# Multiplying the dense tiles of a graph layer in pairs, by halves of columns, and spreading the second products

## The chip, the cores and the metric

The kernel runs on one core of one Trainium2 chip. The metric is the device time of the whole program in microseconds (us). Before the change it is 1784.06 us, the median of three runs (1779.79 to 1784.26).

## What is computed

Two graph layers over N = 2500 nodes with 1024 features and E = 80000 edges, sorted by destination. Both layers see the same edges.

```python
edge_index = jnp.stack([src, dst])
h = jnp.maximum(_layernorm(x, axis=-1), 0.0)
x = x + _L0_gnn_ref(h, L0_gnn_W, edge_weight, src, dst)
h = jnp.maximum(_layernorm(x, axis=-1), 0.0)
x = x + _L1_gnn_ref(h, edge_index, L1_gnn_W, L1_gnn_b)
```

Layer 0 is `support = h @ W`, and then for every edge `support[src]` times its weight, summed by `dst`. Layer 1 is `h @ W.T + b`, and then a sum over the edges and a loop at each node, each scaled by the inverse roots of the degrees of its two ends. All is float32.

## The kernel before

Nodes are cut into 20 tiles of 128 rows. `direct` (L47) works in three stages.

**First stage (up to L526).** Support is multiplied tile by tile on TensorE (`product`, L278) and stored to DRAM. In between the edges are counted (`count_group`, L416): one-hot matrices on VectorE (L436, L438), small bf16 products on TensorE (L440), added to a count matrix per tile of destinations (L448). A tile's counts (20 x 128 x 128 numbers of 16 bits) are stored by SP to `cnat` (L497), and a fresh `counts` buffer is cleared by ScalarE (L422); there are three such buffers. For the first four tiles (`DENSE = 4`; those with most edges) the edge weights are summed in the same way into a matrix `dense[t]` that stays in SBUF.

**Middle stage (L527 to L668).** It forms the sums of layer 0. The 16 thin tiles are gathered (`gathered`, L564): for each block of 128 edges POOL gathers 128 rows of support by an indirect DMA into a buffer `msg` (L569), VectorE makes a one-hot `oh_r` (L573), ScalarE the rounded weighted rows `hi` (L575), VectorE the rest `lo` (L577), and TensorE takes four products (L581). There are 378 such blocks. The four dense tiles are multiplied (`multiplied`, L590): for each of the 20 tiles k of support POOL loads its rows (L595) into a `msg` buffer, and TensorE takes two products of `dense[t]`, one for each half of the columns (L597). `msg` has eight buffers in all, for gathers and dense rows together, and POOL issues in program order.

When a tile's sum is complete, `finish` (L540) adds x to it, stores the sum to DRAM (`x1_d`, L544), normalises it (`normed`, L137), transposes it on TensorE (L534, copied from the PSUM tile `pT` by ScalarE at L535) and multiplies it by the second weights (L554, 16 products, the "second products"), adds the bias (L558) and stores the result to `hid_d` (L561). `finish` is a generator of 12 pieces.

The order is written out by hand. `plan` (L608 to L621) is a list of steps, True for a dense step and False for a block of gathers: `OPENING = 8` dense steps first, and then for each thin tile its blocks with a share of the dense steps among them, two kept for the tile's end; the dense steps end 48 blocks before the end. The tiles come in the order of `ORDER`, so the dense ones as 3, 2, 1, 0. The loop at L640 takes one step after the other, loads the second weights (L646, eight loads of 512 KB on SP) in the first eight steps after the opening, and takes pieces of the tiles that wait in `waiting` at a rate fixed for each thin tile (L620). After each step `count` (L501) may add counting work, from rough costs per engine (`takes`, L467). A framework then lays down one instruction order for each engine and the waits between them; each engine runs its order strictly.

PSUM has two buffers each of `mm` (the sums of a tile, two banks), of `pT` and of `cb` (counts). The tiles of `xt` and `hn` have two buffers each.

**Last stage (from L671).** The degrees, and then for each of the 20 tiles the sum over all tiles of `hid_d` with the transposed counts (L725).

Of the kernel before, what the change touches and what calls it, by code (L numbers as in the profile page):

```python
# [9 lines left out]
F32 = mybir.dt.float32  # L10
# [9 lines left out]
P = 128  # L20
# [7 lines left out]
TILE_BLOCKS = (146, 62, 48, 41, 36, 33, 30, 28, 27, 25, 24, 23, 22, 21, 21, 20, 20, 19, 19, 10)  # L28
# [4 lines left out]
DENSE = 4  # L33
# [4 lines left out]


OPENING = 8  # L40
TAIL = 48

ORDER = (3, 4, 5, 6, 2, 7, 8, 9, 1, 10, 11, 12, 13, 0, 14, 15, 16, 17, 18, 19)
# [3 lines left out]
def direct(  # L47
# [26 lines left out]
    nc = tc.nc  # L74
    N, D = x.shape
    E = src.shape[0]
    NT = -(-N // P)
    KC = D // P
    H = D // 2
# [9 lines left out]
    def rows(t):  # L89
        return min(P, N - t * P)  # L90
# [3 lines left out]
    support = dram.tile([N, D], F32, name="support")  # L94
    cnat = dram.tile([NT, NT, P, P], F16, name="cnat")
    x1_d = [dram.tile([P, D], F32, name=f"x1_d{t}") for t in range(NT)]
# [22 lines left out]
    work = first.enter_context(tc.tile_pool(name="work", bufs=2))  # L119
    psum = first.enter_context(tc.tile_pool(name="psum", bufs=2, space=bass.MemoryType.PSUM))  # L120
# [26 lines left out]
    def load_rows(t, pool):  # L147
        xt = pool.tile([P, D], F32, name="xt")
        if rows(t) < P:
            nc.vector.memset(xt, 0.0)  # L150
        nc.sync.dma_start(xt[:rows(t), :], x[t * P:t * P + rows(t), :])
        return xt
# [69 lines left out]
    start = prep.tile([NT, 1], F32, name="start")  # L222
# [28 lines left out]
    for c in range(QC):  # L251
        n = min(P, NBP - c * P)
# [13 lines left out]
    def on_pe(i):  # L266
        nonlocal last_pe
        last_pe = i
        if len(fences) >= BEHIND and fences[-BEHIND] is not None:
            order_behind(i, fences[-BEHIND])  # L270
        return i
# [27 lines left out]
    for i, to in enumerate((row_p, src_p, wgt_p)):  # L299
        for c0 in range(0, QC, 4):  # L300
            ps = psum.tile([P, 4, P], F32, name="pT")
            m = min(4, QC - c0)
            for c in range(c0, c0 + m):
                n = min(P, NBP - c * P)
                if i == 2:
                    v = got[:n, c, :, 2].bitcast(F32)
                else:
                    v = got_f[:n, i, c, :]
# [7 lines left out]
            for c in range(c0 + whole, c0 + m):  # L316
                n = NBP - c * P
# [11 lines left out]
    for t in range(2, NT):  # L329
        n = TILE_BLOCKS[t] // 2  # L330
        v = second[:, K0[t] - K0[2]:K0[t] - K0[2] + 2 * n].rearrange("p (n g) -> p n g", g=2)
# [81 lines left out]
    dense = {}  # L413
# [53 lines left out]
    def takes(pe=0.0, v=0.0, s=0.0):  # L467
        for i, us in enumerate((pe, v, s)):
            clock[i] += us
        clock[PE] = max(clock[PE], clock[V] - LEAD, clock[S] - LEAD)  # L470
        for i in (V, S):
            clock[i] = max(clock[i], clock[PE] - LEAD)
# [40 lines left out]
    def count_all(t):  # L513
        for queue in to_count:
            while any(g[0] == t for g in queue):
                count_next(queue)
# [13 lines left out]
    def transposed(v, into):  # L530
        for k0 in range(0, KC, 4):
            pT = psum.tile([P, 4, P], F32, name="pT")
            for k in range(4):
                nc.tensor.transpose(pT[:, k, :], v[:, (k0 + k) * P:(k0 + k + 1) * P], ident)  # L534
            nc.scalar.copy(into[:, k0:k0 + 4, :], pT)  # L535
            yield 0.7, 0.0, 0.6

    PIECES = 12

    def finish(t, sums):  # L540

        xt = load_rows(t, work)
        nc.vector.tensor_add(xt, sums.rearrange("p h d -> p (h d)"), xt)  # L543
        nc.sync.dma_start(x1_d[t], xt)  # L544
        yield 0.0, 1.25, 0.0
        hn = normed(xt, work)
        yield 0.0, 2.2, 1.5
        vT = work.tile([P, KC, P], F32, name="vT")
        yield from transposed(hn, vT)
        hid = work.tile([P, D], F32, name="hn")  # L550
        for h in range(2):
            mm = psum.tile([P, 4, P], F32, name="pT").rearrange("p a b -> p (a b)")
            for k in range(KC):
                on_pe(nc.tensor.matmul(mm, vT[:, k, :], w1_sb[k][:, h * H:(h + 1) * H],  # L554
                                       start=(k == 0), stop=(k == KC - 1)))
                if k % 2 and k < KC - 1:
                    yield 1.75, 0.0, 0.0
            nc.vector.tensor_add(hid[:, h * H:(h + 1) * H], mm, bias[:, h * H:(h + 1) * H])  # L558
            if h == 0:
                yield 1.75, 0.65, 0.0  # L560
        nc.sync.dma_start(hid_d[t], hid)  # L561
        yield 1.75, 0.65, 0.0

    def gathered(t, sums):  # L564
        n = TILE_BLOCKS[t]
        for j in range(n):
            k = K0[t] + j
            msg = gpool.tile([P, D], F32, name="msg", bufs=8)
            nc.gpsimd.indirect_dma_start(  # L569
                out=msg, out_offset=None, in_=support,  # L570
                in_offset=bass.IndirectOffsetOnAxis(ap=src_p[:, k:k + 1], axis=0))
            oh = gpool.tile([P, P], F32R, name="oh_r", bufs=3)
            nc.vector.tensor_scalar(oh, iota, row_p[:, k:k + 1], None, op0=ALU.is_equal)  # L573
            hi = gpool.tile([P, D], F32R, name="hi")
            nc.scalar.activation(hi, msg, AF.Copy, scale=wgt_p[:, k:k + 1])  # L575
            lo = gpool.tile([P, D], F32R, name="lo")
            nc.vector.scalar_tensor_tensor(lo, msg, wgt_p[:, k:k + 1], hi.bitcast(F32),  # L577
                                           op0=ALU.mult, op1=ALU.subtract)
            for v in (hi, lo):
                for h in range(2):  # L580
                    i = nc.tensor.matmul(  # L581
                        sums[:, h, :], oh, v[:, h * H:(h + 1) * H],
                        start=(j == 0 and v is hi), stop=(j == n - 1 and v is lo))
                    if v is hi and h == 0:
                        on_pe(i)
            yield 0.92, 1.47, 1.16

    last_load = None

    def multiplied(t, sums):  # L590
        nonlocal last_load
        count_all(t)
        for k in range(NT):
            msg = gpool.tile([P, D], F32, name="msg", bufs=8)
            last_load = nc.gpsimd.dma_start(msg[:rows(k), :], support[k * P:k * P + rows(k), :])  # L595
            for h in range(2):
                i = nc.tensor.matmul(  # L597
                    sums[:, h, :], dense[t][:rows(k), k, :], msg[:rows(k), h * H:(h + 1) * H],
                    start=(k == 0), stop=(k == NT - 1))
                if h == 0:  # L600
                    on_pe(i)
            yield 1.75, 0.0, 0.0

    thick, thin = [t for t in ORDER if t < DENSE], [t for t in ORDER if t >= DENSE]
    blocks = sum(TILE_BLOCKS[t] for t in thin)
    plan = [True] * OPENING  # L608
    rate = [0.0] * OPENING
    done = 0  # L610
    for t in thin:
        n = TILE_BLOCKS[t]
        done += n
        m = min(DENSE * NT, OPENING + -(-(DENSE * NT - OPENING) * done // (blocks - TAIL))) - sum(plan)
        inner = max(m - 2, 0)
        for j in range(n):
            plan.append(False)
            plan += [True] * ((j + 1) * inner // n - j * inner // n)
        plan += [True] * (m - inner)
        rate += [1.1 * PIECES * (1 + m / NT) / (n + m)] * (n + m)  # L620
    assert sum(plan) == DENSE * NT  # L621

    waiting = []
    todo = left(to_count[1])
    w1_sb = []

    def steps_of(tiles):
        for t in tiles:
            sums = psum.tile([P, 2, H], F32, name="mm")
            n = NT if t < DENSE else TILE_BLOCKS[t]  # L630
            for j, took in enumerate((multiplied if t < DENSE else gathered)(t, sums)):
                if j == n - 1:
                    rest = finish(t, sums)
                    takes(*next(rest))
                    waiting.append(rest)
                yield took

    kinds = {True: steps_of(thick), False: steps_of(thin)}
    pieces = 0.0
    for i, is_dense in enumerate(plan):  # L640
        took = next(kinds[is_dense])
        if i == OPENING:
            for k in range(KC):
                w1_sb.append(wpool.tile([P, D], F32, name=f"w{k}"))
        if i >= OPENING and (i - OPENING) < KC:
            order_behind(nc.sync.dma_start(w1_sb[i - OPENING], w1t[(i - OPENING) * P:(i - OPENING + 1) * P, :]),  # L646
                         last_load)
        if i == OPENING + KC:
            nc.sync.dma_start(bias, b1.rearrange("(o d) -> o d", o=1).to_broadcast([P, D]))
        pieces = min(pieces + rate[i], 2.0) if waiting else 0.0  # L650
        while pieces >= 1 and waiting:
            piece = next(waiting[0], None)
            if piece is None:
                waiting.pop(0)
                continue
            takes(*piece)
            pieces -= 1
        count(*took, least=todo * (1 - 1.05 * (i + 1) / len(plan)))
    for steps in kinds.values():
        for _ in steps:  # L660
# [2 lines left out]
        while queue:  # L663
            count_next(queue)
    store_counts(late=False)
    for rest in waiting:
        for _ in rest:
            pass  # L668

# [401 lines left out]
```

## Time and profile before

| What | Value |
|---|---|
| Median of three runs | 1784.06 us |
| The profiled execution, its own time | 1785.47 us |
| Its span | 1783.5 us |
| TensorE busy | 1675.6 us (94%) |
| VectorE busy | 1205.6 us (68%) |
| ScalarE busy | 903.1 us (51%) |
| POOL busy | 537.5 us (30%) |
| Middle stage, from the first dense product to the first product of the last stage | 476.0 to 1398.7 us |
| TensorE, VectorE, POOL busy in the middle stage | 857.7, 760.4, 517.9 us of 922.7 |
| Moved by DMA in the middle stage | 282 MB, 305 GB/s |
| Mean granted TensorE clock, whole span | 0.978 |

A line of a group of instructions gives the source line, the engine, the operation, what is written and read, the shape and the count, and then the busy time and the mean duration of one. A float32 product of 512 columns is recorded as two. "Idle before" is the time the engine had nothing to run ahead of these instructions, with what ended it. In the chain of waits each row is a start, a duration and what ran, followed back from the last instruction of the program to what released it.

### The profile page before, as it was taken

What the parts mean: (1) busy time and instruction counts of PE and PEld (TensorE: products, weight loads), DVE (VectorE), ACT (ScalarE), POOL (GpSimd) and SP (SyncE); (2) the same over time, 40 slices, a digit from 0 to 9 for tenths busy, and PEclk for the clock granted to TensorE, in tenths of its full rate; (3) what the DMA queues carried; (4) which work ended last, traced back from release to release, by engine and by line L of the source; (5) the groups of instructions that cost most, each with busy time, mean ns of one, the idle gap of its engine ahead of it and who ended that gap; (6) DMA issues with size and microseconds to landing.
All of it is one profiled execution on the core that took longest, in us unless ns stands there. A gap on an engine that the chain in (4) does not pass through costs nothing. (4 is left out here: it accounts for less than half of the span.)

```text
span 1783.5 us, 21221 instructions
## 1 busy us (share of the span) xinstructions
PE 1675.6 (94%) x6506; PEld 1039.3 (58%) x6506; DVE 1205.6 (68%) x3051; ACT 903.1 (51%) x1476; POOL 537.5 (30%) x537
## 2 busy tenths in 40 slices
PE   6999999999978998998999889999999999999997
PEld 2465555544345555554555545555565568888886
DVE  5888888898779887788999898777787420000000
ACT  3499999961156655455555444555564431111110
POOL 3000000000257755565656545555562000000000
PEclk9999999999989999999999999999999999999999
DMA  7513122132689988898889888988986773342420
GB/s 248 200 38 94 54 78 60 40 96 71 210 306 358 347 306 280 294 332 277 321 306 337 283 289 266 356 309 316 318 300 215 224 197 93 90 102 80 113 62 32
DMA packets 217424, 369.94 MB, mean 207 GB/s; under 512 B 115758, under 2 KB 135224, under 8 KB 217302
## 3 DMA queue, kind: packets, MB, share of 16 engines
q0 software_dynamic: 66160, 240.22, 38.5%
q1 hardware_dynamic: 151142, 128.29, 23.7%
q8 instruction: 53, 0.87, 0.2%
q14 instruction: 69, 0.57, 0.1%
HBM read 300.79 MB, written 54.56 MB: 199 GB/s over the span
## 5 line engine op out<-in xcount | busy, mean ns | idle before, releaser
L575 ACT ACTIVATE hi<-msg,wgt_p 128x1024 fp32r<-128x1024 f32 x378 | 426.4, 1147 | 359.8 <-PE mm L581 272.7
L569 POOL DMA_INDIRECT msg<-support,src_p x378 | 477.0, 1262 | 325.6 <-DVE lo L577 130.6
L577 DVE SCALAR_TENSOR_TENSOR lo<-msg,wgt_p,hi 128x1024 fp32r<-128x1024 f32 x378 | 478.9, 1280 | 79.4 <-ACT hi L575 47.2
L281 PE MATMUL mm<-w,hT 128*128 128x512 f32 x640 | 317.2, 608 | 2.4 <-ACT hT L173 2.4
L581 PE MATMUL mm<-hi,oh_r 128*128 128x512 f32 x756 | 292.6, 468 | 13.4 <-ACT hi L575 11.5
L554 PE MATMUL pT<-w,vT 128*128 128x512 f32 x640 | 301.3, 593 | 0.0
L581 PE MATMUL mm<-lo,oh_r 128*128 128x512 f32 x756 | 279.3, 450 | 18.3 <-DVE lo L577 18.1
L445 ACT ACTIVATE wl<-oh_low,wpart 128x128 bf16<-128x128 bf16 x891 | 261.8, 403 | 0.0
L725 PE MATMUL mm<-lo,bT 128*128 128x512 f32 (+1 forms) x800 | 248.3, 393 | 3.8 <-DVE lo L699 3.7
L725 PE MATMUL mm<-hi,bT 128*128 128x512 f32 (+1 forms) x800 | 247.9, 392 | 3.1 <-ACT bT L707 2.0
L713 DVE SCALAR_TENSOR_TENSOR rows<-mm,dis,rows 128x1024 f32<-128x1024 f32 x20 | 25.7, 1284 | 307.9 <-PE mm L725 307.9
L581 PEld LDWEIGHTS mm<-lo,oh_r 128*128 128x128 f32 x756 | 139.5, 194 | 102.2 <-DVE lo L577 55.6
L581 PEld LDWEIGHTS mm<-hi,oh_r 128*128 128x128 f32 x756 | 143.1, 193 | 95.4 <-issue 44.9
L438 DVE TENSOR_SCALAR oh_key<-iota,key 128x200 bf16<-128x200 f16 (+12 forms) x675 | 195.1, 292 | 3.0 <-PE cb L452 2.8
L597 PE MATMUL mm<-msg,dense 128*128 128x512 f32 (+1 forms) x320 | 164.4, 631 | 30.1 <-DMA msg<-support 29.6
L707 ACT CAST bT<-cT 128x2560 fp32r<-128x2560 f16 x20 | 46.6, 2335 | 261.2 <-PE mm L725 257.7
L554 PEld LDWEIGHTS pT<-w,vT 128*128 128x128 f32 x640 | 120.5, 189 | 94.7 <-issue 81.3
L725 PEld LDWEIGHTS mm<-lo,bT 128*128 128x128 f32 (+1 forms) x800 | 149.7, 188 | 39.8 <-DVE lo L699 9.0
L725 PEld LDWEIGHTS mm<-hi,bT 128*128 128x128 f32 (+1 forms) x800 | 150.4, 189 | 36.5 <-ACT bT L707 2.4
L436 DVE TENSOR_SCALAR oh_low<-iota,low 128x128 bf16<-128x128 f16 x675 | 168.7, 254 | 3.5 <-PE cb L440 2.2
L448 DVE TENSOR_TENSOR counts<-cb,counts 128x200 f32 (+13 forms) x296 | 138.8, 470 | 41.7 <-PE cb L440 35.4
L281 PEld LDWEIGHTS mm<-w,hT 128*128 128x128 f32 x640 | 109.2, 195 | 65.1 <-issue 59.3
(142 smaller groups left out, 1189.5 us busy)
## 6 DMA issues: line engine op xcount, KB each, us to landing
msg<-support POOLq DMA_DIRECT2D x76, 512.0 KB, 7.1
xt<-in_x SPq DMA_DIRECT2D x38, 512.0 KB, 6.6
cnat<-counts SPq DMA_DIRECT2D x20, 640.0 KB, 9.3
x_d<-xt SPq DMA_DIRECT2D x20, 512.0 KB, 6.5
hid_d<-hn SPq DMA_DIRECT2D x20, 512.0 KB, 6.3
rows<-hid_d SPq DMA_DIRECT2D x20, 512.0 KB, 4.4
rows<-x_d SPq DMA_DIRECT2D x20, 512.0 KB, 4.0
hT<-in_xT SPq DMA_DIRECT2D x19, 512.0 KB, 4.2
```

Source lines behind the costliest of these rows:

```text
L281: on_pe(nc.tensor.matmul(mm[:, h, :], vT[:, k, :], ws[k][:, h * H:(h + 1) * H], start=(k == 0), stop=(k == KC - 1)))
L436: nc.vector.tensor_scalar(oh_low, iota16[:, :P], low[:, k:k + 1], None, op0=ALU.is_equal)
L438: nc.vector.tensor_scalar(oh_key[:, :NT * w], iota16[:, :NT * w], key[:, k:k + 1], None, op0=ALU.is_equal)
L445: nc.scalar.activation(wl[:, i, :], oh_low, AF.Copy, scale=wpart[:, i, k:k + 1])
L448: nc.vector.tensor_tensor(to, cb[:, :NT * w].rearrange("p (t w) -> p t w", w=w), to, op=ALU.add)
L554: on_pe(nc.tensor.matmul(mm, vT[:, k, :], w1_sb[k][:, h * H:(h + 1) * H], start=(k == 0), stop=(k == KC - 1)))
L569: nc.gpsimd.indirect_dma_start(out=msg, out_offset=None, in_=support, in_offset=bass.IndirectOffsetOnAxis(ap=src_p[:, k:k + 1], axis=0))
L575: nc.scalar.activation(hi, msg, AF.Copy, scale=wgt_p[:, k:k + 1])
L577: nc.vector.scalar_tensor_tensor(lo, msg, wgt_p[:, k:k + 1], hi.bitcast(F32), op0=ALU.mult, op1=ALU.subtract)
L581: i = nc.tensor.matmul(sums[:, h, :], oh, v[:, h * H:(h + 1) * H], start=(j == 0 and v is hi), stop=(j == n - 1 and v is lo))
L597: i = nc.tensor.matmul(sums[:, h, :], dense[t][:rows(k), k, :], msg[:rows(k), h * H:(h + 1) * H], start=(k == 0), stop=(k == NT - 1))
L725: nc.tensor.matmul(mm[:, h, :], bT[:rows(k), k, :], v[:rows(k), h * H:(h + 1) * H], start=(k == ORDER[0] and v is his[k]), stop=(k == ORDE ...
```

## The change

Dense tiles are taken in pairs, (3, 2) and then (1, 0). For each half of the columns, one `sums` tile in PSUM holds both tiles' halves; POOL loads two tiles of support rows, half as wide, into one `msg` buffer (for the last two, where rows are fewer, in two loads), and each loaded row is multiplied by both tiles' matrices. At the end of each half x is loaded in halves, added, and stored to `x1_d` in halves. The normalising of these tiles loads `x1_d` again.

`finish` ends with the transposes, and the second products become a generator of their own, `second_rows`. The loop takes second products at a rate set anew for each thin tile from what is pending, and, apart from that, parts of the next tile's normalising (`preparing`) at most every second step. The plan puts 20 dense steps, not 16, before the end of the first thin tile.

```diff
@@ -38,6 +38,7 @@
 
 
 OPENING = 8
+BESIDE = 12
 TAIL = 48
 
 ORDER = (3, 4, 5, 6, 2, 7, 8, 9, 1, 10, 11, 12, 13, 0, 14, 15, 16, 17, 18, 19)
@@ -535,18 +536,27 @@
             nc.scalar.copy(into[:, k0:k0 + 4, :], pT)
             yield 0.7, 0.0, 0.6
 
-    PIECES = 12
-
-    def finish(t, sums):
-
-        xt = load_rows(t, work)
-        nc.vector.tensor_add(xt, sums.rearrange("p h d -> p (h d)"), xt)
-        nc.sync.dma_start(x1_d[t], xt)
-        yield 0.0, 1.25, 0.0
+    PIECES = 8
+
+    def finish(t, sums=None):
+
+
+        if sums is None:
+            xt = work.tile([P, D], F32, name="xt")
+            nc.sync.dma_start(xt, x1_d[t])
+        else:
+            xt = load_rows(t, work)
+            nc.vector.tensor_add(xt, sums.rearrange("p h d -> p (h d)"), xt)
+            nc.sync.dma_start(x1_d[t], xt)
+            yield 0.0, 1.25, 0.0
         hn = normed(xt, work)
         yield 0.0, 2.2, 1.5
         vT = work.tile([P, KC, P], F32, name="vT")
         yield from transposed(hn, vT)
+        products_left.append(second_rows(t, vT))
+
+    def second_rows(t, vT):
+
         hid = work.tile([P, D], F32, name="hn")
         for h in range(2):
             mm = psum.tile([P, 4, P], F32, name="pT").rearrange("p a b -> p (a b)")
@@ -587,57 +597,91 @@
 
     last_load = None
 
-    def multiplied(t, sums):
-        nonlocal last_load
-        count_all(t)
-        for k in range(NT):
-            msg = gpool.tile([P, D], F32, name="msg", bufs=8)
-            last_load = nc.gpsimd.dma_start(msg[:rows(k), :], support[k * P:k * P + rows(k), :])
-            for h in range(2):
-                i = nc.tensor.matmul(
-                    sums[:, h, :], dense[t][:rows(k), k, :], msg[:rows(k), h * H:(h + 1) * H],
-                    start=(k == 0), stop=(k == NT - 1))
-                if h == 0:
-                    on_pe(i)
-            yield 1.75, 0.0, 0.0
+    def multiplied(ts):
+
+
+        nonlocal last_load, pending
+        for t in ts:
+            count_all(t)
+        for h in range(2):
+            sums = psum.tile([P, 2, H], F32, name="mm")
+            cols = slice(h * H, (h + 1) * H)
+            for k0 in range(0, NT, 2):
+                msg = gpool.tile([P, 2, H], F32, name="msg", bufs=8)
+                if rows(k0 + 1) == P:
+                    last_load = nc.gpsimd.dma_start(
+                        msg, support[k0 * P:(k0 + 2) * P, cols].rearrange("(k p) d -> p k d", p=P))
+                else:
+                    for k in (k0, k0 + 1):
+                        last_load = nc.gpsimd.dma_start(msg[:rows(k), k - k0], support[k * P:k * P + rows(k), cols])
+                for k in (k0, k0 + 1):
+                    for i, t in enumerate(ts):
+                        m = nc.tensor.matmul(sums[:, i, :], dense[t][:rows(k), k, :], msg[:rows(k), k - k0],
+                                             start=(k == 0), stop=(k == NT - 1))
+                        if i == 0:
+                            on_pe(m)
+                    if k == NT - 1:
+                        xt = work.tile([P, 2, H], F32, name="xt")
+                        for i, t in enumerate(ts):
+                            nc.sync.dma_start(xt[:, i], x[t * P:(t + 1) * P, cols])
+                        nc.vector.tensor_add(xt, sums, xt)
+                        for i, t in enumerate(ts):
+                            nc.sync.dma_start(x1_d[t][:, cols], xt[:, i])
+                        takes(v=1.25)
+                        if h == 1:
+                            stored.extend(ts)
+                            pending += PIECES * len(ts)
+                    yield 1.75, 0.0, 0.0
+
 
 
 
     thick, thin = [t for t in ORDER if t < DENSE], [t for t in ORDER if t >= DENSE]
     blocks = sum(TILE_BLOCKS[t] for t in thin)
     plan = [True] * OPENING
-    rate = [0.0] * OPENING
+    stretch = [0] * OPENING
     done = 0
     for t in thin:
         n = TILE_BLOCKS[t]
         done += n
-        m = min(DENSE * NT, OPENING + -(-(DENSE * NT - OPENING) * done // (blocks - TAIL))) - sum(plan)
+        begun = OPENING + BESIDE
+        m = min(DENSE * NT, begun + -(-(DENSE * NT - begun) * (done - TILE_BLOCKS[thin[0]])
+                                      // (blocks - TAIL - TILE_BLOCKS[thin[0]]))) - sum(plan)
         inner = max(m - 2, 0)
         for j in range(n):
             plan.append(False)
             plan += [True] * ((j + 1) * inner // n - j * inner // n)
         plan += [True] * (m - inner)
-        rate += [1.1 * PIECES * (1 + m / NT) / (n + m)] * (n + m)
+        stretch += [n + m] + [0] * (n + m - 1)
     assert sum(plan) == DENSE * NT
 
-    waiting = []
+    waiting, stored, products_left = [], [], []
+    pending = 0
     todo = left(to_count[1])
     w1_sb = []
 
-    def steps_of(tiles):
+    def blocks_of(tiles):
+        nonlocal pending
         for t in tiles:
             sums = psum.tile([P, 2, H], F32, name="mm")
-            n = NT if t < DENSE else TILE_BLOCKS[t]
-            for j, took in enumerate((multiplied if t < DENSE else gathered)(t, sums)):
-                if j == n - 1:
+            for j, took in enumerate(gathered(t, sums)):
+                if j == TILE_BLOCKS[t] - 1:
                     rest = finish(t, sums)
                     takes(*next(rest))
                     waiting.append(rest)
+                    pending += PIECES
                 yield took
 
-    kinds = {True: steps_of(thick), False: steps_of(thin)}
-    pieces = 0.0
+    def rows_of(tiles):
+        for i in range(0, DENSE, 2):
+            yield from multiplied(tiles[i:i + 2])
+
+    kinds = {True: rows_of(thick), False: blocks_of(thin)}
+    pieces = rate = parts = 0.0
+    preparing = None
     for i, is_dense in enumerate(plan):
+        if stretch[i]:
+            rate = min(pending - (3 if i + stretch[i] < len(plan) else 0), 14) / stretch[i]
         took = next(kinds[is_dense])
         if i == OPENING:
             for k in range(KC):
@@ -647,14 +691,22 @@
                          last_load)
         if i == OPENING + KC:
             nc.sync.dma_start(bias, b1.rearrange("(o d) -> o d", o=1).to_broadcast([P, D]))
-        pieces = min(pieces + rate[i], 2.0) if waiting else 0.0
-        while pieces >= 1 and waiting:
-            piece = next(waiting[0], None)
-            if piece is None:
-                waiting.pop(0)
-                continue
-            takes(*piece)
-            pieces -= 1
+        pieces = min(pieces + rate, 2.0)
+        while pieces >= 1 and products_left:
+            takes(*next(products_left[0]))
+            pieces, pending = pieces - 1, pending - 1
+            if pending % PIECES == 0:
+                assert next(products_left.pop(0), None) is None
+        parts = min(parts + 0.7, 1.0)
+        if parts == 1 and preparing is None and len(products_left) < 2 and (waiting or stored):
+            preparing = waiting.pop(0) if waiting else finish(stored.pop(0))
+        if parts == 1 and preparing is not None:
+            part = next(preparing, None)
+            if part is None:
+                preparing = None
+            else:
+                takes(*part)
+                parts = 0.0
         count(*took, least=todo * (1 - 1.05 * (i + 1) / len(plan)))
     for steps in kinds.values():
         for _ in steps:
@@ -663,7 +715,11 @@
         while queue:
             count_next(queue)
     store_counts(late=False)
-    for rest in waiting:
+    assert not stored
+    for rest in [preparing] * (preparing is not None) + waiting:
+        for _ in rest:
+            pass
+    for rest in products_left:
         for _ in rest:
             pass
 
```

## The prediction

> **What bounds the kernel now.** I read the page first: busy time, then the span in 40 slices.
>
> ```profile
> PE 1675.6 (94%) x6506; PEld 1039.3 (58%) x6506; DVE 1205.6 (68%) x3051; ACT 903.1 (51%) x1476; POOL 537.5 (30%) x537
> ...
> PE   6999999999978998998999889999999999999997
> ...
> DMA  7513122132689988898889888988986773342420
> ```
>
> TensorE is busy 94% of the span, and the missing tenths lie in slices 11 to 25 and later, just where the DMA row stands at 8 and 9. That is the middle stage, from the first dense product at 476.0 us to the first product of the last stage at 1398.7 us. The view of waits, of PE alone between 445 and 1400 us (total, times, longest), names what ended its idle time:
>
> ```profile
> PE mm L597 <- DMA msg<-support: 29.6, 9, 6.1
> PE mm L581 <- DVE lo L577: 18.1, 45, 2.1
> PE mm L581 <- ACT hi L575: 11.5, 3, 8.5
> ```
>
> So nine waits for dense rows are the largest share; then many small waits for VectorE's `lo`; then one of 8.5 us. The busy time by stretches (columns: PE, PEld, DVE, ACT, POOL, granted clock, DMA share, GB/s) prices the whole stage:
>
> ```profile
> 510.00:520.00 10.00, 7.66 (x21) 5.31 (x21) 6.75 (x8) 7.50 (x7) 5.64 (x4) 0.61 0.49 155
> ...
> 650.00:742.00 92.00, 81.82 (x275) 49.31 (x274) 73.52 (x145) 47.21 (x45) 52.27 (x44) 0.94 0.82 283
> 742.00:823.00 81.00, 76.83 (x257) 45.07 (x256) 73.53 (x141) 45.77 (x42) 52.33 (x43) 0.98 0.90 309
> ...
> 909.00:997.00 88.00, 86.19 (x299) 51.03 (x298) 82.35 (x172) 46.95 (x45) 50.32 (x44) 1.00 0.87 301
> ...
> 476.00:1262.00 786.00, 725.39 (x2381) 423.25 (x2380) 660.37 (x1236) 415.78 (x394) 459.74 (x401) 0.96 0.89 312
> 1262.00:1398.70 136.70, 132.31 (x431) 78.05 (x430) 100.05 (x151) 77.36 (x77) 58.13 (x49) 0.99 0.80 270
> ```
>
> Idle: 922.7 - (725.4 + 132.3) = 65 us. The clock is below 1 in most stretches; (1 - clock) times length over the eleven stretches of the stage (0.92 to 1.00) comes to 29 us of lost TensorE speed. No engine is full: VectorE is at 660/786 = 84% up to 1262 us, DMA at 89%. The chain shows how a row comes late:
>
> ```profile
> 1162.99 0.94 PE mm L581 x4
> 1163.96 0.51 DVE oh_r L573
> 1164.71 0.94 POOL msg L569
> 1166.24 1.22 POOL msg L569
> 1167.46 0.52 issue
> 1167.98 7.36 DMA msg<-support
> 1175.38 1.12 PE mm L597 x2
> ```
>
> A buffer of `msg` comes free, POOL first issues the gathers that stand before the dense row, then the row, and 7.36 us of transfer are left bare. The issues of the stage (size, median us to landing):
>
> ```profile
> msg<-support POOLq DMA_DIRECT2D x68, 512.0 KB, 7.1
> ...
> hid_d<-hn SPq DMA_DIRECT2D x20, 512.0 KB, 6.3
> xt<-in_x SPq DMA_DIRECT2D x17, 512.0 KB, 6.8
> cnat<-counts SPq DMA_DIRECT2D x10, 640.0 KB, 16.2
> ```
>
> The wait of 8.5 us is another matter: ACT, in order, was to clear a `counts` buffer (L422) whose store had not landed, and the gathers' `hi` stood behind it:
>
> ```profile
> 498.67 1.15 ACT L575 ACTIVATE hi<-msg,wgt_p 128x1024 fp32r<-128x1024 f32 x1 [0.24 <-DVE lo L577]
> 508.49 2.32 ACT L422 CAST counts<-zero 128x2560 f16<-128x2560 f32 x1 [8.66 <-DMA cnat<-counts]
> ```
>
> **What the Trainium skill says.** "TensorE: Matmul & The Clock Gate", Part 1: an idle window of some 3.4 us puts the array at half clock until it has been busy again. The trace agrees: the gap of 8.5 us that ends at 511.9 us is followed by the stretch at clock 0.61. "DMA: Bandwidth & Descriptors", Issuing engines are not separate DMA queues: what SP and POOL issue interleaves on the same 16 engines; so rows saved on POOL's queue also speed SP's stores. The same page, Specifications: below 512 B a transfer loses its rate. The counts store has runs of 256 B, and 640 KB take 16.2 us where 512 KB in long runs take 6.3 to 6.8; half rows of 2 KB stay above that bound. The same page, Two DMAs through the same engine are not ordered: a read of what a DMA wrote has to wait for its semaphore. No run yet shows this; it prices the new reload.
>
> **The change part by part.** Everything is set against the profiled execution: 1785.5 us, of which 1783.5 span and 2 around it; the median of the runs shown is 1784.06, 1.4 us less.
>
> *Arithmetic.* In the order of the changed program TensorE has the same 160 dense products, 320 second products, 1512 gather products and 160 transposes in this stage; VectorE's and ScalarE's counts are equal too. At the chain's full-speed durations (a dense or second product 6.88/8 = 0.86 us, since each is recorded twice, a gather product 1.85/8 = 0.23, eight transposes 0.87, a count product about 0.155) that is 808 us before and after. So only waits can change.
>
> *Dense rows.* 80 loads of up to 512 KB (41 MB) become 44 issues with half the bytes (20.5 MB): 7% of the stage's 282 MB, 53 us of transfer at 390 GB/s (512 KB per 1.3 us in the saturated stretch around 550 us). One load now feeds four products, 3.4 us of TensorE, instead of 1.7, and every second step needs none. A loaded pair holds its buffer over two steps, so POOL's lead of eight buffers isn't longer. Of 29.6 us I leave 6: -24 (0 to -29.6). POOL's 36 issues fewer, at 0.57 us, are hidden: POOL is busy 56%.
>
> *Clock.* With most gaps over 3 us gone, I take 18 of the 29 us back: -18 (0 to -29).
>
> *Opening.* SP now queues all eight loads of the second weights ahead of that counts store, where three stood behind it: 1.5 MB, +4 us. Against it five dense loads fewer compete (2.6 MB, -6.7 us), and two or more dense steps stand ahead of the waiting products. Net -2 (-8 to +8).
>
> *The dense tiles' sums go through DRAM.* Each half is stored and x1 loaded again (4 loads more, 2 MB: nothing in bytes). The reload waits for the store: 1.2 (add) + 0.4 + 6.5 + 6.6 = about 15 us from sum to statistics. VectorE's order has 10 us of work between them for the first pair, 3 us for the second; `oh_r` and `lo` queue behind the statistics, and TensorE waits for those. For the second pair I allow 4 us of products as cover: 8 us of wait; the first is covered nearly. +8 (0 to +18). On SP the next x load and a hidden store stand behind the reload; both are wanted more than 20 us later.
>
> *Second products spread.* Transposes now fall inside an open accumulation that holds one of two `pT` banks, so a tile's second four wait for ACT's copy (0.58 us) of the first four; other products stand between in most tiles: +4 (0 to +12). And there is a shift: by gather 324 of 378 the old order has done 240 second products, the new one 211. With the dense products equal (154), TensorE has 25 us less to do up to there and 25 us more after it.
>
> Sum: -24 - 18 - 2 + 8 + 4 = -32; 1785.5 - 32 = 1753.5, on the runs' scale 1752.
>
> **A second reckoning** from the shift. The last 54 gathers and the tail are TensorE's: 128 us of products before (measured 136.7), 153 after, so about 159: +22, and the reload's +8. All gain must come from the first 324 gathers, 786 us now. TensorE has 654 us there and VectorE still 660, so VectorE's share decides: at 91% they take 725, total -31; at 87% 759, total +3. Stretches without much waiting for rows reached 91% (742 to 823) and 94% (909 to 997), that with the worst waits 80% (650 to 742).
>
> **Rivals.**
> *Deeper:* the waits for rows, the half clock and the opening go nearly whole, and reload and transposes are hidden: -29 - 29 - 8 = -66, 1718. Against it: 18 us of small waits for `lo` have nothing to do with rows.
> *Given back:* the rows arrive, but TensorE then waits for VectorE: at 88% the first part takes 750, so -36 + 30 = -6, 1779. For it: VectorE must do about 70 us of work per 36 gathers in the early part, where TensorE's share falls to 60 to 68.
> *Slower:* second products are put off without the early part getting shorter. Place: gathers 36 to 144, where the new order has done 50 second products and the old 80, 26 us. If the gathers there run at their old pace, bound by VectorE, POOL's eight buffers and latency, the 22 us come back at the end with nothing beside them. At 85.5% the first part takes 772: -14 + 30 = +16, 1801. It decides from 756 us for the first 324 gathers upward.
> *Not as it says:* that the pairing is missing is excluded by the program's order: 44 row issues.
>
> **How the numbers follow.** Forecast (1736 to 1772): 0.50, likeliest value 1752. Deeper, 1718: 0.12. Given back, 1779: 0.20, of which 0.08 ends faster, 0.11 within and 0.01 slower than the bound of 0.3% (5.4 us, about what a measurement of this kernel can tell from no change). Slower, 1801: 0.18. So faster 0.70, same 0.11, slower 0.19. The range 1720 to 1792 takes in the forecast, the given-back case, half the deeper and a part of the slower one.
>
> **What would show it.** Right: waits of PE for dense rows under 10 us in all; the clock of the stage above 0.98; first 324 gathers in about 725 us; the tail after them longer, near 165. A wait of VectorE's statistics for the reload near the last dense sums, some 8 us on TensorE. Wrong: row waits as before (buffers, not bytes, were short), or waits for `lo` far above 18 us (VectorE was the bound), or a longer wait behind the counts store at the opening.

## The result, and the profile after

The changed kernel takes 1754.04 us (median of six runs, 1751.36 to 1761.22) against 1783.76 us before (six runs, 1779.79 to 1790.94): a ratio of 0.9838, 95% interval 0.9812 to 0.9865. The profiled execution takes 1753.3 us with a span of 1751.5, where the one before took 1785.47: -32.2 us, forecast -32.

The page after (busy time, then two rows of the 40 slices):

```profile
PE 1660.9 (95%) x6506; PEld 1031.8 (59%) x6506; DVE 1202.0 (69%) x3051; ACT 907.1 (52%) x1476; POOL 526.8 (30%) x501
...
PE   6999999999988699989999999999899999999997
...
DMA  8513212132489889898888898998774763433420
```

TensorE, VectorE and ScalarE have as many instructions as before, POOL 36 fewer. TensorE's slices 15 to 25 are now mostly 9, but there is a new 6 in slice 14. Waits of TensorE between 445 and 1400 us (total, times, longest):

```profile
PE mm L591 <- ACT hi L585: 19.5, 6, 10.9
PE mm L591 <- DVE lo L587: 14.3, 19, 6.1
PE mm L591 <- DVE mv L135: 5.3, 1, 5.3
...
PE mm L619 <- DMA msg<-support: 2.5, 3, 1.6
```

The waits for dense rows, 29.6 us before, are 2.5. The waits for `hi` have grown from 11.5 to 19.5, and two long ones on VectorE are new: 5.3 and, among those for `lo`, 6.1. The stretches up to gather 324, after it, and the whole stage (PE, PEld, DVE, ACT, POOL busy, clock, DMA share, GB/s):

```profile
477.00:1201.00 724.00, 684.11 (x2312) 404.02 (x2311) 651.28 (x1225) 416.78 (x389) 450.70 (x368) 0.98 0.89 310
1201.00:1365.60 164.60, 157.53 (x501) 89.73 (x499) 105.94 (x163) 80.37 (x81) 57.90 (x50) 0.98 0.71 237
477.00:1365.60 888.60, 841.65 (x2811) 493.76 (x2810) 757.23 (x1387) 497.15 (x470) 508.60 (x418) 0.98 0.85 296
```

724 and 164.6 us, where the second reckoning had 725 and "near 165". The stage is 34 us shorter: 18 us less idle (65 to 47) and 16 us less busy time for the same products. By the clock column (0.97 of 922.7 us before, 0.98 of 888.6 now) some 10 of these 16 are the clock; what shortened the rest is not shown.

The new 6 in slice 14, on ScalarE, and the reload, on VectorE in two windows:

```profile
592.21 1.15 ACT L585 ACTIVATE hi<-msg,wgt_p 128x1024 fp32r<-128x1024 f32 x1 [0.47 <-DVE lo L587]
603.46 2.32 ACT L423 CAST counts<-zero 128x2560 f16<-128x2560 f32 x1 [10.09 <-DMA cnat<-counts]
```

```profile
783.25 1.29 DVE L133 BATCH_NORM_STATS2 stats<-xt 128x6 f32<-128x512 f32 x2 [4.51 <-DMA xt<-x_d]
...
1231.01 1.29 DVE L133 BATCH_NORM_STATS2 stats<-xt 128x6 f32<-128x512 f32 x2 [7.25 <-DMA xt<-x_d]
```

The clear of a `counts` buffer waited 10.1 us for the store of what it held before. SP issued that store only at 577.3 us, although its counts were complete by 552.3: the program holds each such store back by six steps, and before it on SP stood the new stores of the dense sums and loads of x, one of which waited 7.5 us for a store. And both pairs' statistics waited for their reload, the second for 7.25 us: stores issued at 1218.5 and 1218.9, the reload at 1225.0, the statistics at 1231.0. This is what the Trainium skill ("DMA: Bandwidth & Descriptors", Two DMAs through the same engine are not ordered) led one to expect: a read of what a DMA wrote has to wait for that DMA's semaphore. The trace agrees: before this reload SP waited 5.2 us for the stores.

### The profile page after: what moved, and what is told of

Read it like the earlier page. It is cut to its first block, busy times and chain, and to the rows that moved or that the text cites. A ratio compares the mean times of both kernels' runs of the same rounds, so it can differ in the third digit from the quotient of the medians.

```text
span 1751.5 us, 21194 instructions
## 1 busy us (share of the span) xinstructions
PE 1660.9 (95%) x6506; PEld 1031.8 (59%) x6506; DVE 1202.0 (69%) x3051; ACT 907.1 (52%) x1476; POOL 526.8 (30%) x501
## 5 line engine op out<-in xcount | busy, mean ns | idle before, releaser
L591 PE MATMUL mm<-lo,oh_r 128*128 128x512 f32 x756 | 295.8, 472 | 15.1 <-DVE lo L587 14.3
L564 PE MATMUL pT<-w,vT 128*128 128x512 f32 x640 | 308.2, 594 | 0.0
L591 PE MATMUL mm<-hi,oh_r 128*128 128x512 f32 x756 | 281.6, 454 | 24.8 <-ACT hi L585 19.5
L619 PE MATMUL mm<-msg,dense 128*128 128x512 f32 (+1 forms) x320 | 156.5, 603 | 2.6 <-DMA msg<-support 2.5
L441 PE MATMUL cb<-oh_key,oh_low 128*128 128x200 bf16 (+12 forms) x675 | 139.4, 289 | 8.3 <-DVE oh_key L439 5.6
```

Of the source, the lines that this page charges most:

```text
L441: last_count = nc.tensor.matmul(cb[:, :NT * w], oh_low, oh_key[:, :NT * w], start=(k == a), stop=(k == b - 1))
L591: i = nc.tensor.matmul(sums[:, h, :], oh, v[:, h * H:(h + 1) * H], start=(j == 0 and v is hi), stop=(j == n - 1 and v is lo))
L619: m = nc.tensor.matmul(sums[:, i, :], dense[t][:rows(k), k, :], msg[:rows(k), k - k0], start=(k == 0), stop=(k == NT - 1))
```

## The experiments

The sum had come out, so the question was whether its reasons hold. The theory of the prediction: half the bytes and fewer loads make the rows come in time. The rival: the even rate of second products does it. All ratios are to the kernel before, run on the same chip.

**One half of the change at a time.** `schedule_only` keeps the new plan, `second_rows` and the rate, but takes dense tiles one at a time:

```diff
     def multiplied(ts):
...
-        for h in range(2):
             sums = psum.tile([P, 2, H], F32, name="mm")
...
+            for k in range(NT):
+                msg = gpool.tile([P, D], F32, name="msg", bufs=8)
+                last_load = nc.gpsimd.dma_start(msg[:rows(k), :], support[k * P:k * P + rows(k), :])
...
```

> The changed kernel's plan, its separate second products and their even rate, but the dense tiles one at a time with whole rows: 80 loads of 512 KB, no stored sums. Theory (the gain is fewer bytes and requests for dense rows, hence shorter waits for rows and less half clock): the waits for rows stay at 20 to 35 us, the clock near 0.96 to 0.97, and the time is 1775 to 1795. Rival 'even rate' (the gain is the spread of the second products): the waits for rows fall below 12 us without pairing and the time is 1745 to 1762. In both there is no wait of the statistics for a reload.

Measured: 1756.25 us, ratio 0.9832 (0.9791 to 0.9872). Waits of TensorE in its middle stage:

```profile
PE mm L591 <- ACT hi L585: 26.3, 5, 9.9
PE mm L591 <- DVE lo L587: 8.8, 19, 1.1
...
PE mm L609 <- DMA msg<-support: 2.0, 2, 1.5
```

The theory fails here: with all 80 loads of whole rows, 300.8 MB read as before, the waits for rows are gone and the whole gain is there. `pairs_only` is the other half: the changed `multiplied` in the plan and with the 12 pieces of before.

> The plan and the pieces of the kernel before, but the dense tiles in pairs by halves of columns: 44 loads, half the bytes, sums stored and reloaded. Theory: waits for rows under 10 us, the time 1750 to 1768, with one or two waits of 5 to 12 us for the reload that nothing spreads. Rival 'even rate': no gain or little without the schedule, 1775 to 1795, because second products then come in clumps and VectorE's lo is waited for.

Measured: 1752.65 us, 0.9813 (0.9764 to 0.9861), waits of TensorE:

```profile
PE mm L585 <- DVE lo L581: 19.2, 33, 5.3
PE mm L613 <- DMA msg<-support: 15.5, 8, 4.5
PE mm L585 <- ACT hi L579: 7.0, 1, 7.0
```

The rival fails too: pairing alone also brings the whole gain, though half of the waits for rows are still there. Each half is enough, and both together are worth no more than one.

**Bytes in the new schedule.** `whole_rows` is the changed kernel with a load of 512 KB for every step; `single_rows` has one of 256 KB for every step. The edit of `whole_rows`, shortened:

```diff
-                msg = gpool.tile([P, 2, H], F32, name="msg", bufs=8)
-                    last_load = nc.gpsimd.dma_start(msg, support[k0 * P:(k0 + 2) * P, cols]...)
                 for k in (k0, k0 + 1):
+                    msg = gpool.tile([P, D], F32, name="msg", bufs=8)
+                    last_load = nc.gpsimd.dma_start(msg[:rows(k), :], support[k * P:k * P + rows(k), :])
```

> The changed kernel, but every dense step loads the whole row of 512 KB into a buffer of its own although it uses one half of the columns: 80 loads, the traffic of the kernel before, in the changed order. Theory (bytes and requests): waits for rows back to 20 to 35 us and the time 1773 to 1790. Rival 'even rate': waits for rows stay under 12 us, the time within 5 us of the changed kernel (1750 to 1760).

> The changed kernel with one load of 256 KB for each dense step, each in a buffer of its own: half the bytes as in the changed kernel, but 80 loads and a lead of eight steps as before. If the bytes decide: waits for rows 2 to 10 us and the time 1750 to 1762. If the number of loads and the lead in buffers decide: waits for rows above 18 us and the time 1770 to 1788. In between (1762 to 1770) both count.

Measured: 1750.11 us, 0.979 (0.9749 to 0.9831), with no wait for rows that the view lists; and 1756.73 us, 0.9827 (0.9786 to 0.9868), with 16.2 us of them in 11 waits:

```profile
PE mm L614 <- DMA msg<-support: 16.2, 11, 4.2
```

In the new schedule twice the bytes cost nothing, and half the bytes in 80 buffers had more waits for rows than the whole rows. Neither bytes nor the number of loads decides here.

**Why rows were late.** So what do the waits of before have in common? For each dense row I took the time from its issue on POOL to its use. The seven rows that were waited for by more than 2 us had 7.1 to 8.9 us of it, the wait included, which is just what their transfers took; most of the others had 10 to 18. The five longest waits of before; each window runs from the issue of the row to its product, and counts only TensorE's second products (instructions with `vT`: busy time, clock, DMA share, GB/s):

```profile
663.30:671.30 8.00, 0.00 (x0) 1.00 0.92 306
716.10:725.00 8.90, 0.00 (x0) 0.87 1.01 406
829.00:837.70 8.70, 0.00 (x0) 0.86 1.00 308
1006.20:1013.30 7.10, 0.00 (x0) 0.97 1.07 362
1061.60:1069.00 7.40, 0.00 (x0) 0.89 1.02 390
```

In none of them is there a second product. In POOL's order a buffer of `msg` comes free eight fetches before its next content is used; if only gathers (0.92 us of TensorE each) and one row lie between, eight fetches are some 8.2 us of work (7 x 0.92 + 1.75), and a row's transfer has a median of 7.1. These five had still less: TensorE was busy for 4.5, 4.5, 2.9, 3.1 and 1.3 us of the windows, because its own order takes each of these rows ahead of all products of three or four gathers that POOL had issued before it. In the last window it waited for the row until 1069.0 us, while `lo` of one of those gathers was ready at 1065.8. Of the 64 dense rows after the opening (the first 16), 12 had under 7 us between issue and use, the wait not counted.

The rate of before, `1.1 * PIECES`, runs out of pieces ahead of the next tile, and I took this for the reason. In the order of the instructions 13 of these 64 rows have no second product among the eight fetches ahead of them, in `schedule_only` none of 59. But of the seven late rows only two are among these 13; before the others second products do stand among the eight fetches, but all of them, or all but one, were done before POOL issued the row. A rival is open too: in the five windows DMA is all but full (0.92 to 1.07), so that a full DMA may make the rows late, and second products in between would thin out the loads as well. Against it stands that the rows issued at 829.6 and 830.2 us took 10.7 and 11.4 us to land and were not waited for, with 16.7 and 18.0 us to their use. By either reason it should help to spread the second products, and one constant does that:

```diff
-        rate += [1.1 * PIECES * (1 + m / NT) / (n + m)] * (n + m)
+        rate += [0.95 * PIECES * (1 + m / NT) / (n + m)] * (n + m)
```

> The kernel before with one constant changed: the rate of the pieces of second products, 1.1 to 0.95, so that they no longer run out ahead of the next tile. In its order 3 of 64 dense rows (13 before) have no second product among the eight fetches ahead of them. Theory 'lead' (a row comes late where only gathers lie between its issue and its use, so that eight buffers are 7 to 9 us of TensorE's work): waits for rows fall from 29.6 us to under 12 and the time to 1762 to 1776, some 7 us of the gain given back as the tail has 8 second products more. Theory 'bytes' (the traffic of whole rows makes them late): waits for rows stay at 20 to 35 us and the time at 1780 to 1790.

Measured: 1754.82 us, 0.9813 (0.9778 to 0.9847), better than expected. Waits of TensorE, then second products between issue and use of five of its rows, the third the only one that was waited for by more than 2 us:

```profile
PE mm L581 <- ACT hi L575: 22.8, 5, 9.2
PE mm L581 <- DVE lo L577: 14.0, 32, 1.3
PE mm L597 <- DMA msg<-support: 4.4, 4, 2.6
```

```profile
674.10:690.30 16.20, 2.90 (x7) 0.76 0.63 252
714.50:724.80 10.30, 3.76 (x8) 1.00 0.98 370
818.20:824.10 5.90, 0.00 (x0) 1.00 1.01 342
1006.40:1021.30 14.90, 3.99 (x8) 1.00 0.95 339
1068.90:1083.00 14.10, 7.39 (x16) 1.00 0.82 266
```

The waits for rows fall from 29.6 to 4.4 us with every byte still moved, at a DMA share of the stage of 0.90 against 0.88. Of the 64 rows 3 have under 7 us between issue and use, the wait not counted, where there were 12. One constant gives what the whole change gave. It is shown that the even rate, and not fewer bytes, takes the waits for rows away; whether by the longer lead, by TensorE's order or by a DMA that is full less often is not separated. An edit of TensorE's order alone was not run.

**Bytes in the old schedule.** `pairs_whole` is `pairs_only` with a whole row loaded at each step:

> Pairs by halves in the plan and with the pieces of the kernel before, but each step loads the whole row of 512 KB into a buffer of its own: the traffic and number of loads of the kernel before, with pairing's order and stored sums alone left. Theory 'bytes' for the pairing's gain: waits for rows back to 25 to 40 us and the time 1778 to 1792. Rival (the pairing gains by its order: dense sums that are stored need no normalising at once, and so on): the time stays at 1750 to 1760.

Measured: 1783.1 us, 0.9988 (0.9966 to 1.0009): without its smaller traffic, or its fewer buffers, pairing gains nothing. But not by the waits expected:

```profile
PE mm L585 <- DVE lo L581: 27.0, 49, 7.4
PE mm L585 <- ACT hi L579: 15.3, 4, 7.2
PE mm L608 <- DMA msg<-support: 13.7, 8, 4.6
```

The waits for rows are as in `pairs_only` (15.5). What differs is `lo`, +7.8 (2.1 of it the wait for the reload, 7.4 against 5.3), `hi`, +8.3, and 12.5 us of busy time for the same products (853.3 against 840.8). Part of it is again the store of counts: ScalarE's clears wait 17.7 us for it, against 11.0. So in the old schedule the dense loads cost something other than waits for rows. Whether by their bytes or by the buffers that they take was not separated there, and the path of the 30 us is only seen in part.

**The new waits.** `late_stats` normalises a stored tile at the earliest six steps after its sums and issues the reload two parts ahead of the statistics; `free_store` stores the counts as soon as they are done:

```diff
-            to_store.append([6, t])
+            to_store.append([1, t])
-            if late:
-                order_behind(i, last_pe)
```

> The changed kernel, but a stored dense tile is normalised only six steps after its sums were stored, and its reload is issued two parts ahead of the statistics. Theory (the two waits of VectorE's statistics for the reload leave TensorE bare for 5.3 and 6.1 us): both gaps go, the time falls by 8 to 14 us against the changed kernel, to 1740 to 1746. Rival (those gaps are slack that another wait takes over, or the pieces come later and lengthen the tail): less than 3 us, 1751 to 1757.

> The changed kernel, but the two stores of counts that ScalarE's clearing waits for are issued on SP as soon as their counts are done: the first ahead of most of the second weights, the second ahead of the dense sums' stores and the loads of x that stood before it. Theory (gaps of 3.8 us at 504 and of 10.9 us at 596 on TensorE are the clear's wait for a store held up on SP, the second of them made by the change): both go, 10 to 18 us less than the changed kernel, 1736 to 1744. Rival (TensorE at 596 then waits for the same gathered rows, or the store delays the weights or x by as much): less than 4 us, 1750 to 1757.

> Both edits together: stored dense tiles normalised later, counts stored at once. If the four gaps are independent: the sum of both gains and the half clock behind the gaps, 20 to 30 us less than the changed kernel, 1724 to 1734. If one covers the other: no better than the better of the two, 1738 to 1744.

Measured: `late_stats` 1751.62 us, 0.9803 (0.9776 to 0.983), its interval overlapping that of the changed kernel; `free_store` 1777.58 us, 0.9957 (0.9938 to 0.9975); both together 1775.61 us, 0.9946 (0.9926 to 0.9966). Neither theory nor rival foresaw a loss. In `late_stats` the first wait went and 5.6 us of the second stayed, since the statistics were still moved up to the reload; the waits for rows rose from 2.5 to 10.4 us beside it. (Its trace is of the slowest of its six executions, 1758.97 us.) In `free_store` the waits for `hi` doubled, and ScalarE shows why:

```profile
PE mm L589 <- ACT hi L583: 38.7, 8, 10.5
...
553.93 2.32 ACT L423 CAST counts<-zero 128x2560 f16<-128x2560 f32 x1 [9.66 <-DMA cnat<-counts]
666.71 2.32 ACT L423 CAST counts<-zero 128x2560 f16<-128x2560 f32 x1 [8.27 <-DMA cnat<-counts]
774.35 2.32 ACT L423 CAST counts<-zero 128x2560 f16<-128x2560 f32 x1 [7.93 <-DMA cnat<-counts]
862.02 2.32 ACT L423 CAST counts<-zero 128x2560 f16<-128x2560 f32 x1 [8.90 <-DMA cnat<-counts]
```

Each store is issued at once, and each clear has followed it: it still waits 8 to 10 us. The scheduler that orders each engine's instructions seems to put a clear as early as it thinks the buffer free, and the store takes longer than that; this is read from the orders that it made. In the changed kernel the clear of 603.5 us serves a tile whose counting begins at 762.0. So not the store was to be moved but the clear:

```diff
-            nc.scalar.copy(counts[t]..., zero.to_broadcast([P, NT * P]))
+            clear = nc.scalar.copy(counts[t]..., zero.to_broadcast([P, NT * P]))
+            if last_pe is not None:
+                order_behind(clear, last_pe)
```

> The changed kernel with one dependence of order more: ScalarE's clear of a counts buffer is kept behind the TensorE step at which its tile's counting begins, where the scheduler had put it as early as the buffer came free, just behind that buffer's store. Theory (the waits of TensorE for hi, 19.5 us in all, are ScalarE standing before these clears): they fall under 4 us, the half clock behind them goes too, and the time is 1728 to 1740. Rival (the counting begins later and VectorE waits for the clear instead, or the gathers are bound by VectorE or rows at those places anyway): 1748 to 1757.

> The schedule alone (dense tiles one at a time, whole rows, no stored sums) with the clears pinned as in the other kernel. Its waits for hi were 26.3 us. If the clears are those waits: 1722 to 1738, and then the pairing is worth nothing beside the schedule, or less than nothing because of the two reloads. If pairing's smaller traffic shows once the clears no longer wait: 5 to 15 us slower than the pinned changed kernel. Rival: no gain, 1748 to 1758.

Measured: `pin_after` 1743.11 us, 0.9761 (0.974 to 0.9782); `pin_schedule` 1729.18 us, 0.969 (0.967 to 0.971). The first is 3 us outside what was expected. Waits of TensorE, `pin_after` and then `pin_schedule`:

```profile
PE mm L593 <- DVE lo L589: 14.9, 17, 7.4
PE mm L593 <- DVE mv L135: 5.9, 1, 5.9
PE mm L621 <- DMA msg<-support: 4.5, 3, 3.1
...
PE mm L593 <- ACT hi L587: 1.2, 1, 1.2
```

```profile
PE mm L593 <- DVE lo L589: 8.2, 15, 2.1
PE pT L537 <- ACT hn L145: 7.8, 4, 2.2
PE mm L611 <- DMA msg<-support: 5.1, 5, 2.6
...
PE mm L593 <- ACT hi L587: 2.3, 3, 1.4
```

The waits for `hi` were the clears: 19.5 and 26.3 us become 1.2 and 2.3. The pinned changed kernel's stage is 19 us shorter (869.5), but begins 6.7 us later, probably because the clears of the first stage are pinned too. And pairing is now 14 us worse than no pairing. The 5.9 and 7.4 us are its reloads, so the last kernel adds to `pin_after` the delay of `late_stats`, and keeps the statistics behind TensorE's step as well:

```diff
-        hn = normed(xt, work)
+        hn = normed(xt, work, last_pe if sums is None else None)   # order_behind of the bn_stats
```

> The pinned changed kernel, and beside it a stored dense tile is normalised at least six steps after its sums were stored, with its statistics kept behind the TensorE step at which they are wanted, so that no statistics stand on VectorE ahead of a reload that has not landed. Theory (the 14 us by which the pinned changed kernel is slower than the pinned schedule alone, 1743 against 1729, are its two waits for the reload, 5.9 and 7.4 us on TensorE, with the half clock behind them): both waits go and the time is 1727 to 1735. Rival (the 14 us lie elsewhere: in the order of the tail, or in later second products): 1739 to 1746.

Measured: 1724.96 us, 0.9667 (0.9635 to 0.9699), the fastest of all. Waits, and its whole middle stage:

```profile
PE mm L597 <- DVE lo L593: 9.4, 21, 2.3
PE mm L625 <- DMA msg<-support: 4.1, 3, 2.9
...
PE mm L597 <- ACT hi L591: 1.6, 3, 1.2
```

```profile
483.70:1334.60 850.90, 829.63 (x2806) 488.47 (x2806) 753.20 (x1376) 499.39 (x471) 504.09 (x418) 1.00 0.89 310
```

Both reload waits are gone. The stage is 18.6 us shorter than in `pin_after`: 11 less idle (32 to 21) and 7.5 less busy time for the same products (837.1 to 829.6), at a clock of 1.00 against 0.98; no idle time of TensorE there is longer than 2.9 us. So the 14 us were the reloads (13.3 us of waits) and what a slower clock cost behind them. Against `pin_schedule` pairing is then 4 us ahead, with intervals that overlap.

## Why the prediction was right

| Step | Forecast | Measured |
|---|---|---|
| Dense rows | -24 | 29.6 to 2.5: -27.1 |
| Clock | -18 | busy time of the same products 857.7 to 841.65: -16, of which the clock column gives 10 |
| Opening (store of counts) | -2 | `hi` 11.5 to 19.5: +8 |
| Reload of the dense sums | +8 | 5.3 + 6.1 = +11.4 |
| Second products spread | +4 | small waits for `lo` 18.1 to 14.3 - 6.1 = 8.2, transposes +1.1: -9 |
| Sum | -32 | -32.5, of -34.1 in the stage and -32.2 in all |

**Dense rows.** The size was right, the reason stated for it only half. "80 loads of up to 512 KB (41 MB) become 44 issues with half the bytes" was given as the cause, with the remark that POOL's lead isn't longer. `whole_rows` and `even_before` show that bytes and loads did not decide: with all of them left the waits went, once the second products were spread. In buffers the lead stayed the same; in time the short ones went (12 rows under 7 us, in `even_before` 3). The trace had these before the run; the prediction read the chain to "POOL first issues the gathers that stand before the dense row" and did not ask how much work lay between issue and use. It also took the 7.36 us of that transfer to be "left bare", where TensorE waited 2.0 us of them. For the old schedule alone, smaller traffic or fewer buffers would have done (`pairs_only` against `pairs_whole`), so the step was not false, but it did not add to the even rate.

**Clock.** The mechanism is right, the size is not: 18 of 29 us were to come back, and by the clock column it is 10 ((1 - 0.97) x 922.7 against (1 - 0.98) x 888.6). That the busy time fell by 16, near the forecast, is in part luck, since the other 6 us have no explanation here. The Trainium skill ("TensorE: Matmul & The Clock Gate", Part 1) ties it to idle windows; here the stage without gaps over 2.9 us (`pin_late_stats`) has a clock of 1.00, that of the changed kernel, with one of 10.9 us, has 0.98.

**Opening.** Half right, and the term has the wrong sign. The named wait fell from 8.5 to 3.8 us, but the next clear met a store that SP had queued behind the stores of dense sums, 10.9 us. The prediction counted what SP is given ahead of the first store and not of the second, though it did reckon with SP's order at the reload.

**Reload.** The mechanism is right, the first pair mis-sized: "covered nearly" was 5.3 us. Its own figures, 15 us from sum to statistics with 10 us of VectorE's work between, leave 5 us of VectorE's wait, and 4.5 came; but it put TensorE's share of them at nearly nothing, although the `lo` and `oh_r` behind the statistics are held up too. The second, forecast 8, was 6.1.

**Second products spread.** The term that failed in sign: transposes were costed (+4, measured 1.1), and the gain in small waits for `lo` was not. Which part of the change brings that gain is not shown: of 18.1 us, `schedule_only` has 8.8 left, the even rate alone (`even_before`) 14.0, and `pairs_only` 13.9 without the 5.3 of its reload.

So the sum held partly by luck: errors of +10, +3 and +2 stood against -13 and -3. The second reckoning, from TensorE's work before and after gather 324, was the sounder one: 724 against 725, and 164.6 against 165, with 157.5 us of products in the tail where 153 were counted. But its parts were loose too. The 91% for VectorE was picked from stretches of 80 to 94%; 90% came (651 of 724), and it is no bound, as `pin_late_stats` reaches 93% (647 of 694 us). And 25 us more on a tail of 136.7 are 162 and not 159, so that with the 8 us of the reload it had 170 rather than 165. Of the rivals, *Slower* was ruled out at its own point: 724 us, far from 756. *Given back* was not seen; but its idea, that a removed wait is followed by another, is true of the clears and the reload: with both held back the changed kernel is 60 us ahead and not 30. What pinned clears would give the kernel before, alone or with `even_before`, was not run.

## What to carry to other kernels

A load's lead in buffers says little; measure the work that lies between its issue and its use, above all where filler work runs out, before cutting its bytes. When an in-order engine waits, look at what the waiting instruction is for: an initialisation that is wanted 158 us later should be held back, and making its releaser earlier only pulls it along. Two edits that remove the same wait do not add up; try each alone, and the smallest of them first.

## What the runs showed that was not expected

DMA's share was no sign of the bound: `pin_schedule` moves 328 GB/s over the stage at a share of 0.93, more than any other, and waits 5.1 us for rows; the kernel before waited 29.6 us at 0.88 and 305 GB/s. The store of counts, 640 KB in runs of 256 B, held up its clear for up to 26 us after its issue (577.3 to 603.5 us) and some 15 us where it was issued at once (538.8 to 553.9). Why `single_rows`, with half the bytes, waits more often for rows than `whole_rows` was not settled.
